# Layer-2 feed-forward: four of a token's six expert rows summed by TensorE, two added by VectorE, none by GpSimd

## The chip, the cores and the metric

The kernel runs on one core of a Trainium2 chip. A core has five engines that work side by side, each with its own queue of instructions that it takes in order: TensorE (PE in the profile, with its weight loads as PEld), VectorE (DVE), ScalarE (ACT), GpSimd (POOL) and SyncE (SP), which here only starts transfers. Transfers run on 16 DMA engines. The on-chip memory for operands is SBUF; TensorE writes its products to PSUM, which has eight banks here, and VectorE and ScalarE read them from there. The metric is the device time of one execution in microseconds (us), taken as the median of several runs.

## The reference, cut to what matters

The program is a stack of four layers on 1024 tokens of 256 numbers (4 sequences of 256), all in 32-bit floating point. Every layer has the form "half a feed-forward, attention, half a feed-forward", each on a normalised copy of the running sum x. The change is in layer 2's feed-forward, which runs twice, before and after layer 2's attention. It is a mixture of 64 experts; each token goes to its six best, and one shared expert takes all tokens:

```python
x = x + 0.5 * _L2_ffn_ref(_layernorm(x), ...)       # and again after the attention

scores = softmax(xf @ gate_w.T)
topk_w, topk_idx = top_k(scores, 6)
# the tokens of each expert are gathered (at most 64 an expert)
gu = einsum('ech,ehi->eci', gx, gate_up_proj)
g, u = split(gu, 2)
eo = einsum('eci,eih->ech', silu(g) * u, down_proj) * buf_w[..., None]
routed = zeros.at[buf_tok].add(eo)                    # six rows a token are added up
shared = (silu(xf @ shared_gate_w.T) * (xf @ shared_up_w.T)) @ shared_down_w.T
return routed + shared
```

So every token ends with x + 0.5 * (the sum of its six expert rows + the shared expert's row). How those six rows are added is what the change is about.

## The kernel before

The running sum lies in SBUF all the time as eight tiles of 128 tokens by 256 numbers, `m.x[0]` to `m.x[7]`; tiles 0 to 3 are half 0, tiles 4 to 7 half 1. `m.xT` holds the normalised and transposed copy of each half, as TensorE's operand. `norm_steps` (L169) makes it: per tile the statistics (`st`, L176, and `mv`, L177), per half a chain of small steps on VectorE for the reciprocal root (`rsqrt`, L155), then per tile the normalised rows `xn` (L185), two transposes by TensorE (L136) and a copy.

`l2_ffn` (L868) works in these steps.

- The norm, the router's scores, the six best experts of a token and the lists of slots.
- Sixteen groups of four experts (`experts`, L954), eight of them in flight at a time: an indirect transfer by GpSimd fetches rows of tokens (L971), TensorE makes the gate and up products (L990) and the down products, and an indirect transfer by GpSimd writes each result row to its place in a table in DRAM, `parts` (L1019). A token's six rows lie side by side there.
- The shared expert (L1028 to L1034), in two halves of 512 tokens: `gated` (L193) makes two blocks of gate and up products and their product `hs` on VectorE (L203); then for each of four tiles a down product of two accumulating steps goes into a PSUM bank `accb` (two such banks), and VectorE adds half of it to x (`add_to_x`, L208, which is L209 in the profile).
- The collection (L1035 to L1045): for each of the eight tiles a transfer on SP's queue reads the 128 x 6 x 256 numbers of `parts` into a buffer `got` (L1037; four buffers), once all scatters have landed. GpSimd adds rows 3, 4 and 5 to rows 0, 1 and 2 in one instruction over 128 x 768 elements (L1043). VectorE then adds half of each of the three remaining rows to x, three `add_to_x` in all.

After the first call comes layer 2's attention (`l2_attn`), which starts with the norm of both halves. After the second call come layer 3's feed-forward and attention, half by half, the second half begun some turns after the first (`staggered`, L1783).

The kernel is written with a framework (Tile) that puts in all semaphores and hands out the buffers. It also sets the order of each engine's queue, once, when the program is built: it plans the whole program with its own estimate of each instruction's duration and takes, for each engine, what it believes to be ready, the earlier written first. No order is written by hand in these lines. On the chip an engine then keeps to this order, even where its next instruction waits and a later one could run. The names of buffers are those of the profile: `got`, `x`, `accb`, `hs`, `parts`.

A product of 32-bit numbers shows in the trace as two instructions of TensorE.

Of the kernel before, what the change touches and what calls it, by code (L numbers as in the profile page):

```python
# [10 lines left out]
F32 = mybir.dt.float32  # L11
# [3 lines left out]
ALU = mybir.AluOpType  # L15
# [4 lines left out]
P = 128  # L20
B, S, D = 4, 256, 256
# [846 lines left out]
def l2_ffn(m, w, tables, beside=None):  # L868
# [4 lines left out]
    nc, io = m.nc, m.io  # L873
    E, K = 64, 6
    table, parts = tables
    with ExitStack() as ctx:
# [72 lines left out]
        wk = pool("l2f", 2)  # L949
# [78 lines left out]
        for half in range(2):  # L1028
            cols = lambda f: slice(f * 96, f * 96 + 96)
            h = m.gated(wk, half, lambda k, f: w.sg[:, k, cols(f)], lambda k, f: w.su[:, k, cols(f)], [96] * 2, "hs")  # L1030
            for q in range(4):
                o = m.acc_bank()
                m.mm(o[:, :D], [(h[f][:96, q * P : (q + 1) * P], w.sd[:, f, :]) for f in range(2)])
                m.add_to_x(half * 4 + q, o[:, :D], 0.5)  # L1034
        for t in range(NT):  # L1035
            got = wk.tile([P, K, D], F32, name="got", bufs=4)
            ins = nc.sync.dma_start(  # L1037
                out=got.rearrange("p k d -> p (k d)"),
                in_=parts[t * K * P : (t + 1) * K * P, :].rearrange("(p k) d -> p (k d)", k=K),
            )  # L1040
            for s in scattered:
                m.tc.add_manual_dep(ins.ins, s.name, written, reason="any expert may have written these rows")
            nc.gpsimd.tensor_tensor(got[:, :3], got[:, :3], got[:, 3:], ALU.add)  # L1043
            for k in range(3):
                m.add_to_x(t, got[:, k], 0.5)  # L1045


def l2_attn_weights(m, wk):
# [684 lines left out]
def program(tc, io):  # L1733
    with ExitStack() as ctx:
# [4 lines left out]
        with tc.tile_pool(name="small2", bufs=1) as small2:  # L1739
            with slots() as m.wts:  # L1740
                with tc.tile_pool(name="small1", bufs=1) as m.small:
                    with tc.tile_pool(name="l1w", bufs=2) as stage:
                        with m.banks(4, 2, 2):
                            with tc.tile_pool(name="l0w", bufs=1) as wk:
                                with tc.tile_pool(name="l0i", bufs=1) as early:
                                    w0, rest = l0_weights(m, wk, early)
                                wa, parts = l1_attn_weights(m, stage)
                                w1 = l1_ffn_weights(m)
                                next(parts)
                                l0_ffn(m, w0, rest)  # L1750
                        with m.banks(0, 2, 2):
                            l0_attn(m, w0, parts)
                    with tc.tile_pool(name="l2w", bufs=1) as stage:
                        m.small = small2
                        m.causal = m.table(stage, "causal")
                        zero = stage.tile([P, D + 64], F32, name="zero")
                        nc.gpsimd.memset(zero, 0.0)
                        (w2, turned), (wb, more) = l2_ffn_weights(m, stage), l2_attn_weights(m, stage)
                        with m.banks(4, 2, 2):
                            l0_ffn(m, w0)  # L1760
                            l1_ffn(m, w1)
                        with m.banks(0, 2, 2):
                            tables = l2_tables(m, zero)
                            l1_attn(m, wa, chain(turned, more))
                    with m.banks(4, 2, 2):
                        l1_ffn(m, w1)
                with m.banks(4, 2, 2):
                    l2_ffn(m, w2, tables[0])
            with m.banks(6, 0, 2):
                l2_attn(m, wb)  # L1770
            with m.banks(4, 2, 2), tc.tile_pool(name="small3", bufs=1) as m.small:
                late = []
                with tc.tile_pool(name="wts", bufs=5) as m.wts:
                    l2_ffn(m, w2, tables[1], lambda: late.extend((l3_ffn_weights(m), l3_attn_weights(m))))
                w, wa = late
                with ExitStack() as pools:
                    pool = lambda name, bufs: pools.enter_context(tc.tile_pool(name=name, bufs=bufs))
                    one, wf, wk = pool("l3a1", 1), pool("l3f", 2), pool("l3a", 4)
                    l3_attn_tables(m, wa, one)
                    layer = lambda half: chain(  # L1780
                        l3_ffn(m, w, wf, half), l3_attn(m, wa, wk, half), l3_ffn(m, w, wf, half)
                    )
                    staggered((layer(half) for half in range(2)), 2, 14)  # L1783
# [40 lines left out]
```

## Time and profile before

| | |
|---|---|
| median of 3 runs | 2099.32 us (2096.6 to 2113.83) |
| the profiled execution, time | 2095.15 us |
| its span, first to last instruction | 2093.4 us |
| TensorE busy (PE) | 1816.7 us, 87% |
| VectorE busy (DVE) | 1198.1 us, 57% |
| ScalarE busy (ACT) | 707.4 us, 34% |
| GpSimd busy (POOL) | 578.1 us, 28% |
| mean granted clock of TensorE | 0.914 of full |
| collection in call 1, first load issued to last add | 964.8 to 999.5 us |
| collection in call 2, first load issued to last add | 1852.7 to 1887.9 us |
| one load of `got`, issue to landing (median) | 4.3 us for 768 KB |

All durations come from one execution, recorded by the hardware profiler. Times in a view count from the start of its span. In a line of the timeline the first number is the start, the second the time that the group took, then come engine, line of the kernel, operation, out<-in, shapes, and how many instructions were merged; in brackets stands how long the engine was idle before it, and what ended that wait. A busy share of an engine is an average over the whole program; what a change in one stage is worth has to be read in that stage. "PEclk" or "granted clock" is the clock that TensorE was allowed, as a share of full speed. The chain of waits names, step by step and backwards from the end, what each piece of work had waited for. A wait for several things is put down to the one that came last.

### The profile page before, as it was taken

Reading aid. Unit: us, or ns where it says so; the run is one execution under the profiler, and the core shown is the slowest. Engines: PE = TensorE matmul, PEld = TensorE weight load, DVE = VectorE, ACT = ScalarE, POOL = GpSimd, SP = SyncE. Lnnn points to the kernel's source line nnn. Section 1 sums busy time; section 2 is a strip of 40 time slices with the busy share of each in tenths; the row PEclk is TensorE's granted clock in tenths of the full one; section 3 lists DMA queues with packets and bytes.
Section 4 is the critical chain, followed back from the end, with each engine's and each line's share of the span. In section 5 each row is a group of like instructions: output and inputs, shape, how many; then the busy total and the mean of one; then the engine's idle time right before and its main releaser. Section 6 shows DMA issues by size and latency. Waiting matters only on the chain. (4 is left out here: it accounts for less than half of the span.)

```text
span 2093.4 us, 33728 instructions
## 1 busy us (share of the span) xinstructions
PE 1816.7 (87%) x12924; PEld 1184.3 (57%) x12924; DVE 1198.1 (57%) x2910; ACT 707.4 (34%) x1573; POOL 578.1 (28%) x1128
## 2 busy tenths in 40 slices
PE   3979999998998999487659999999999967877888
PEld 2445655466556566353336677667777754534555
DVE  8653434333555433545778887788765653464562
ACT  7325521101545211121324554544545531211210
POOL 0023200001323000176334435334333232751110
PEclk9976899999999999698769999999999986988999
DMA  8001002235000213295120111111011045950000
GB/s 232 3 10 41 11 19 61 86 106 167 1 1 1 81 41 81 84 298 194 48 82 22 42 42 52 32 52 37 17 37 38 15 114 153 302 190 0 1 3 18
DMA packets 121872, 147.38 MB, mean 70 GB/s; under 512 B 18008, under 2 KB 95472, under 8 KB 121712
## 3 DMA queue, kind: packets, MB, share of 16 engines
q1 hardware_dynamic: 113488, 123.72, 19.6%
q0 software_dynamic: 6144, 18.88, 2.9%
q10 hardware_dynamic: 2080, 2.62, 0.3%
q8 instruction: 103, 1.69, 0.3%
q14 instruction: 57, 0.47, 0.1%
HBM read 120.03 MB, written 25.17 MB: 69 GB/s over the span
## 5 line engine op out<-in xcount | busy, mean ns | idle before, releaser
L132 PE MATMUL mmb<-xT,slot 128*128 128x512 f32 (+2 forms) x640 | 285.8, 603 | 2.0 <-DVE h L203 1.0
L132 PEld LDWEIGHTS mmb<-xT,slot 128*128 128x128 f32 (+2 forms) x640 | 118.3, 188 | 151.6 <-issue 144.7
L209 DVE SCALAR_TENSOR_TENSOR x<-accb,x 128x256 f32<-128x256 f32 x112 | 47.0, 421 | 195.4 <-PE accb L132 195.3
L132 PE MATMUL accb<-slot,h 128*128 128x256 f32 (+2 forms) x640 | 145.3, 384 | 0.0
L132 PEld LDWEIGHTS accb<-slot,h 128*128 128x128 f32 (+2 forms) x640 | 119.0, 190 | 28.5 <-issue 13.9
L1175 DVE SCALAR_TENSOR_TENSOR qT<-mmb,l_conv,qT 128x510 f32<-128x510 f32 (+2 forms) x96 | 70.8, 738 | 58.5 <-ACT qT L1171 57.6
L590 ACT ACTIVATE sg<-mmb 128x512 f32<-128x512 f32 (+1 forms) x56 | 33.4, 597 | 199.2 <-PE mmb L132 196.3
L144 ACT COPY xT<-trb 128x256 f32<-128x256 f32 x44 | 16.3, 371 | 201.3 <-PE trb L136 175.5
L971 POOL DMA_INDIRECT rows<-table,source x64 | 61.9, 968 | 75.0 <-ACT l_ffn L1549 36.1
L772 POOL TENSOR_TENSOR e<-e,den 128x512 f32<-128x512 f32 x64 | 51.5, 826 | 109.4 <-DVE den L769 106.3
L1175 DVE SCALAR_TENSOR_TENSOR vT<-mmb,l_conv,vT 128x510 f32<-128x510 f32 (+2 forms) x96 | 71.2, 741 | 18.1 <-ACT vT L1171 17.2
L1221 POOL TENSOR_TENSOR put<-lt,t_same 32x128 f32<-32x128 f32 x128 | 63.9, 499 | 27.3 <-DVE lt L1216 20.5
L720 POOL TENSOR_TENSOR x<-x,l_bo 128x256 f32<-128x256 f32 x8 | 6.5, 832 | 230.7 <-DVE xn L185 230.7
L1000 DVE SCALAR_TENSOR_TENSOR h<-sg,rows,mmb 64x96 f32<-64x96 f32 x128 | 40.0, 313 | 50.9 <-ACT sg L995 48.8
L592 DVE TENSOR_TENSOR sg<-sg,c 128x512 f32<-128x512 f32 x44 | 30.8, 701 | 67.0 <-ACT sg L590 51.2
L1019 POOL DMA_INDIRECT parts<-os,target x64 | 63.0, 984 | 19.9 <-issue 12.7
L1175 DVE SCALAR_TENSOR_TENSOR kT<-mmb,l_conv,kT 128x510 f32<-128x510 f32 (+2 forms) x96 | 66.3, 735 | 1.9 <-ACT kT L1171 1.7
L990 PE MATMUL mmb<-slot,gx 128*64 128x192 f32 x512 | 61.7, 361 | 6.3 <-DVE gx L142 5.7
L132 PE MATMUL mmb<-xT,wq 128*128 128x512 f32 x128 | 67.1, 649 | 0.0
L132 PE MATMUL accb<-wo,zT 128*128 128x256 f32 x256 | 60.9, 391 | 6.0 <-DVE x L209 4.4
L132 PE MATMUL mmb<-xT,l_ffn 128*128 128x512 f32 x128 | 64.3, 653 | 1.2 <-DVE xT L142 1.2
L136 PE MATMUL trb<-t_ident,xn 128*128 128x128 f32 x144 | 31.6, 343 | 38.3 <-DVE xn L185 31.3
(452 smaller groups left out, 4336.4 us busy)
## 6 DMA issues: line engine op xcount, KB each, us to landing
slot<-_L_ffn_gate_up_proj_dram SPq DMA_DIRECT2D x16, 1536.0 KB, 8.7
slot<-in_L_ffn_down_proj_dram SPq DMA_DIRECT2D x8, 1536.0 KB, 14.4
parts<-zero SPq DMA_DIRECT2D x16, 768.0 KB, 9.5
got<-parts SPq DMA_DIRECT2D x16, 768.0 KB, 4.3
bca<-scr SPq DMA_DIRECT2D x32, 256.0 KB, 3.1
bcb<-scr SPq DMA_DIRECT2D x32, 256.0 KB, 3.2
c<-rows SPq DMA_DIRECT2D x16, 256.0 KB, 3.2
table<-xs ACTq DMA_DIRECT2D x2, 1280.0 KB, 5.1
```

The source lines that it names most:

```text
L132: self.nc.tensor.matmul(out=out, lhsT=a, rhs=b, start=i == 0, stop=i == last, **kw)
L136: self.nc.tensor.transpose(out, in_, self.ident[:n, :n])
L209: self.nc.vector.scalar_tensor_tensor(self.x[t], got, scale, self.x[t], ALU.mult, ALU.add)
L590: nc.scalar.activation(sg[:n], g[:n], AF.Silu)
L592: nc.vector.tensor_tensor(sg, sg, c, ALU.mult)
L772: nc.gpsimd.tensor_tensor(e[:, :, cut], e[:, :, cut], den[:, i, :].unsqueeze(2).to_broadcast([P, 2, n]), ALU.mult)
L971: nc.gpsimd.indirect_dma_start(out=r, out_offset=None, in_=table, in_offset=bass.IndirectOffsetOnAxis(ap=slot[0][:, 2 * g + i : 2 * g + i ...
L990: nc.tensor.matmul(out=ps[half, i, :], lhsT=xT[:, i, k, half], rhs=gu[:, 4 * (g % 2) + 2 * i + j, k, :], start=k == 0, stop=k == KC - 1,)
L1000: nc.vector.scalar_tensor_tensor(h[half, i, :], sg[half, i, :], rows[i][half, D + e : D + e + 1], ps[half, i, 96:], ALU.mult, ALU.mult,)
L1019: ins = nc.gpsimd.indirect_dma_start(out=parts, out_offset=bass.IndirectOffsetOnAxis(ap=slot[1][:, 2 * g + i : 2 * g + i + 1], axis=0), in ...
L1175: nc.vector.scalar_tensor_tensor(yi[:, :, d:], ps[:, :, : S - d], tap(j), yi[:, :, d:], ALU.mult, ALU.add)
L1221: nc.gpsimd.tensor_tensor(batches[b].put[rows(q), :, :, u * G : u * G + G], lt[rows(q), :, rows(q)].rearrange("p c (z t) -> p t z c", z=2) ...
```

## The change

In the collection, GpSimd's addition is taken out. For each tile TensorE now multiplies rows 2, 3, 4 and 5 by the identity matrix (`m.ident`, 128 x 128), all four accumulating in one PSUM bank `accb`; that bank then holds their sum. VectorE adds half of rows 0 and 1 to x, and half of the bank. `got` has five buffers instead of four.

```diff
         for t in range(NT):
-            got = wk.tile([P, K, D], F32, name="got", bufs=4)
+            got = wk.tile([P, K, D], F32, name="got", bufs=5)
             ins = nc.sync.dma_start(
                 out=got.rearrange("p k d -> p (k d)"),
                 in_=parts[t * K * P : (t + 1) * K * P, :].rearrange("(p k) d -> p (k d)", k=K),
             )
             for s in scattered:
                 m.tc.add_manual_dep(ins.ins, s.name, written, reason="any expert may have written these rows")
-            nc.gpsimd.tensor_tensor(got[:, :3], got[:, :3], got[:, 3:], ALU.add)
-            for k in range(3):
+            o = m.acc_bank()
+            m.mm(o[:, :D], [(m.ident, got[:, k]) for k in range(2, K)])
+            for k in range(2):
                 m.add_to_x(t, got[:, k], 0.5)
+            m.add_to_x(t, o[:, :D], 0.5)
```

## The prediction

> **What bounds the kernel now.** The page comes first: TensorE is busy for 87% of the 2093.4 us span, so over the whole kernel it is the bound. The change touches two short stretches only, the ends of the two layer-2 feed-forwards, so I then read the timeline of those (965 to 1008 us, 1852 to 1890 us). The first, with columns start, duration, engine, line, operation, count and, in brackets, the idle time before and its releaser:
>
> ```profile
> 969.31 1.80 POOL L1043 TENSOR_TENSOR got<-got 128x768 f32<-128x768 f32 x1 [5.38 <-DMA got<-parts]
> ...
> 972.10 7.70 POOL L1043 TENSOR_TENSOR got<-got 128x768 f32<-128x768 f32 x4 [0.99 <-DMA got<-parts]
> ...
> 972.41 0.42 DVE L209 SCALAR_TENSOR_TENSOR x<-accb,x 128x256 f32<-128x256 f32 x1
> ...
> 974.19 5.89 DVE L209 SCALAR_TENSOR_TENSOR x<-got,x 128x256 f32<-128x256 f32 x3 [0.62 <-POOL got L1043]
> ...
> 980.68 0.67 DVE L203 TENSOR_TENSOR hs<-sg,mmb 96x512 f32<-96x512 f32 x1
> ...
> 981.40 2.07 PE L132 MATMUL accb<-l_sd,hs 96*128 96x256 f32 x4 [7.15 <-DVE hs L203]
> ...
> 998.07 0.41 DVE L185 TENSOR_SCALAR xn<-x,mv,rs 128x256 f32<-128x256 f32 x1
> ```
>
> Three VectorE adds take 5.89 us, 1.96 us each, exactly while GpSimd's four adds run; an add that reads PSUM in the same stretch takes 0.42. Behind them in VectorE's queue waits the product hs, and TensorE stands for 7.15 us for it. So this stretch is bound by VectorE, and VectorE is held by GpSimd. The spread of the two kinds of add (min/median/max in ns, from the views of the tiles got and accb) says the same:
>
> ```profile
> L209 DVE SCALAR_TENSOR_TENSOR x<-got,x x48: 401/425/2030, 971.1 to 1887.5; 128x256 f32<-128x256 f32 x48
> L1043 POOL TENSOR_TENSOR got<-got x16: 1790/1867/2054, 969.3 to 1878.1; 128x768 f32<-128x768 f32 x16
> ```
> ```profile
> L209 DVE SCALAR_TENSOR_TENSOR x<-accb,x x8: 405/416/424, 965.3 to 991.1; 128x256 f32<-128x256 f32 x8
> ```
>
> The windows (busy time of PE, PEld, DVE, ACT and POOL, then granted clock, DMA share, GB/s) show TensorE without work and its clock at half as a consequence:
>
> ```profile
> 975.00:980.00 5.00, 0.00 (x0) 0.00 (x0) 4.93 (x3) 0.00 (x0) 4.80 (x3) 0.91 0.20 75
> 980.00:985.00 5.00, 2.37 (x5) 1.47 (x6) 4.76 (x13) 0.00 (x0) 0.63 (x1) 0.50 0.69 238
> ```
>
> Last, the waits of the DMA queue: a fifth load waits until an old buffer's adds are done.
>
> ```profile
> SPq L1037 <- DVE x L209: 18.1, 4, 7.1
> ```
>
> **The change, part by part.** Per call there are eight tiles of 128 tokens.
>
> *GpSimd's add goes.* In call 1 the stretched adds are 5.89 us for three (1.28 unstretched, at 425 ns) and 1.89, 1.67 and 1.61 for one each: 4.6 + 1.5 + 1.2 + 1.2 = 8.5 us too long. In call 2 they are 4.32 for three, 1.25, 1.89, 2.95 for three, and two tiny norm steps of 1.71 and 1.76: 3.0 + 0.8 + 1.5 + 1.7 + 1.5 + 1.6 = 10.1 us. The first add of each call also no longer waits for GpSimd's 1.8. The ceiling of this term is 8.5 + 1.8 + 10.1 + 1.8 = 22 us, if nothing else becomes the bound.
>
> *VectorE's own count stays.* Three adds a tile before (three row sums), three after (two rows, one PSUM sum), and a PSUM add costs 416 ns against 425. Nothing.
>
> *TensorE gets 32 products a call*, four a tile, two instructions each. The trace has no product with the identity over 256 columns; the nearest row is the layer-3 down product of the same shape (128x128 by 128x256), 64 instructions in 13.83 us, from the chain; the row at half clock is the shared expert's:
>
> ```profile
> 1905.93 13.83 PE accb L132 x64
> ```
> ```profile
> 1877.72 3.78 PE L132 MATMUL accb<-l_sd,hs 96*128 96x256 f32 x8 [0.56 <-DVE x L209]
> ```
>
> That is 0.216 us an instruction, 1.73 us a tile, 13.8 us a call at full clock; at half clock 0.47, 3.8 a tile, 30 a call. I take the full clock, because with products to do TensorE has no gap as long as the 5 us that halved it at 979; the other end goes to a rival. This is the term that takes most of the ceiling back. The weights' loads (0.19 us) lie beneath the products.
>
> *What the path becomes.* Each engine's queue is in order. In TensorE's, the shared expert's products are written ahead of the identity products and are always ready first, so I expect all eight sums behind them.
>
> Call 1: the gate and up products end at 974.25, as now. VectorE's hs for the second half is queued behind the adds of about four tiles. The loads' landings: first 969.2, second 972.1, and the DMA engines stay full until 975.5, so the fourth is there at about 976. So hs ends at about 977.3; four shared down products at 0.9 us (the rows at full clock) end at 981; four sums end at 988.1, eight at 995.0. From the last add's end to the first normalised tile it takes 0.42 + 3.96 us (statistics at 1000.36 to xn at 1004.32 now). Half 0 is normalised from 992.5 instead of 998.07, half 1 from 999.4 instead of 1004.32: **-5 us**, since layer 2's attention needs both.
>
> Call 2: gate and up end at 1864.9, loads land earlier (the first at 1857.1, four by 1862.3), so hs ends near 1865.5, shared products 1869.4, four sums 1876.3, eight 1883.2. Half 0 could be normalised from 1880.7 instead of 1884.80, but its transposes stand behind the last sums: 1883.3 instead of 1885.27, -2.0. The clock then stays up: layer 3's first products ran at 0.50 from 1890.07 to about 1893.6, which lost 1.8. **-3.8 us**.
>
> *VectorE's two row adds now wait for the load alone.* Now the first three come right behind the first two shared adds, though GpSimd's 1.8 us lies before them. Freed of it they may be queued ahead of these shared adds. A second new wait is the third add's for TensorE's sum; behind it stand hs and the norm's steps, which the sums above include. If the row adds go ahead, the shared adds wait for the landing: 969.2 + 0.85 instead of 965.26, 4.8 us in call 1, and 1857.1 + 0.85 instead of 1855.94, 2.0 us in call 2; TensorE's next shared product waits for the bank. That leaves -0.2 and -1.8. So the two ends are -8.8 and -2.0, and with the queue order unknown I take **-5**.
>
> *The fifth buffer.* A buffer is now freed by TensorE's sum as well, later than by VectorE. From the release to the landing is 4.3 us (median of the load); TensorE takes 6.9 us over the other four, so five buffers hide it and four would (5.2) only just. It costs nothing on the path; with one tile as cover it would be 4.3 - 1.7 = 2.6 us for each of three loads. Queued behind the loads in SP's queue are three small tables in call 1, whose first reader is at 992.7 and off the path.
>
> *Sum.* On the profiled execution: 2095.15 (span 2093.4) - 5 = **2090**. The median of the runs shown, 2099.32, is 4 above it, so a median of 2094 would say the same; that stays inside the range.
>
> [...] The clock: in call 1 TensorE stopped at 974.25 and the granted clock fell at 979.5; in call 2 it stood from 1864.94 to 1868.47, 3.5 us, and the next burst of 1.13 still ran at full clock, with half clock from 1870. [...]
>
> **The rivals.**
> 1. *The queues come out ideally*: hs is not behind late loads, TensorE never waits. From 963.5, 14.5 us of shared work and 6.9 for four sums give 984.9, and half 1's end at 991.7: half 1 is normalised from 996, -8.3; call 2 gets to about -6.5, and the attention starts with the clock up, -1. That is 2079; up to the ceiling of 22, with the queues later in the kernel also falling well, 2073. For it: TensorE is idle for 20 of the 43 us from 965 to 1008. Against it: eight sums make TensorE this stretch's bound.
> 2. *TensorE is the new bound at half clock: slower.* If the first row adds stand ahead of the shared adds, TensorE is idle from about 967 to 970 and again for hs; from a gap above 5 us (the one at 974) the clock is at half, and a tile's sum costs 3.8 instead of 1.73: +2.1 x 8 = 17 us a call until some 4 us of unbroken work restore it (1890.07 to 1893.6). For both calls without restoring +34 - 2 = +32, 2127; with restoring half-way about +15, 2110. For it: the shared down products run at half clock now, in both calls. Against: the sums are unbroken work, once started.
> 3. *The order moves elsewhere.* A new ready time in one stage can change the queues of what follows, 708 us of attention (64 of them without TensorE work) and 203 of layer 3 (31). Either sign; I bound it by a tenth of that idle time gained, and by twice as much lost: -10 to +20, 2080 to 2110.
> 4. *Nothing comes of it*: the sums end when GpSimd's adds did; 2095. The equality of 13.8 us of sums and 8 x 1.8 = 14.4 of GpSimd speaks for it, TensorE's idle time against.
>
> **How the numbers follow.** The forecast, with its own ends of 2086 and 2093, 40; rival 1 and the good half of 3, 19; rival 4, 16; rival 2 and the bad half of 3, 25. The range that leaves out a tenth on each side is 2070 to 2114. A per cent is 21 us, about what a measurement of this kernel tells from no change. Faster by more takes nearly the ceiling plus a better order later: 16 in 100. Slower by more takes half clock in both calls or a worse order later: 20. Within: 64.
>
> **What would show it.** In the profile of the changed kernel no row add should be above 0.45 us, GpSimd's line should be gone, and 64 identity instructions a call should take 13.8 us. If they take near 30, rival 2 holds. The idle time before hs and before the shared down products tells whether row adds stand ahead of them; the starts of xn in both calls give the two terms, and the time from there to the end tells rival 3. The prediction is wrong if that last stretch moves by more than 10 us, or if TensorE takes sums ahead of shared products and waits for loads.

## The result, and the profile after

The changed kernel takes 2109.41 us (median of 20 runs, 2101.41 to 2121.38), the kernel before beside it 2101.61 us (20 runs): a ratio of 1.0036, 95% interval 1.002 to 1.0053. That is 7.6 us slower (4.2 to 11.1), where 5 us faster was forecast. The two profiled executions lie further apart, 2117.6 against 2095.15 us, because one execution is not a median: the stretch ahead of the first call, in which nothing was changed, took 863.1 us in one and 852.8 in the other.

What GpSimd had done to VectorE is gone, as the view of the tile got shows (min/median/max in ns):

```profile
L132 PE MATMUL accb<-got,t_ident x128: 378/379/634, 993.6 to 1910.9; 128*128 128x256 f32 x128
L209 DVE SCALAR_TENSOR_TENSOR x<-got,x x32: 407/424/426, 980.3 to 1909.5; 128x256 f32<-128x256 f32 x32
```

No row add is above 426 ns; before, the longest took 2030. The timeline of the first call, lines of VectorE, TensorE and SP taken together, to be held against the first one shown of before (this execution is 10.8 us later when the shared expert begins):

```profile
976.03 0.86 DVE L209 SCALAR_TENSOR_TENSOR x<-accb,x 128x256 f32<-128x256 f32 x2 [0.79 <-PE accb L132]
...
980.31 0.88 DVE L209 SCALAR_TENSOR_TENSOR x<-got,x 128x256 f32<-128x256 f32 x2 [3.43 <-DMA got<-parts]
981.12 0.42 DVE L209 SCALAR_TENSOR_TENSOR x<-accb,x 128x256 f32<-128x256 f32 x1
...
985.24 0.68 DVE L203 TENSOR_TENSOR hs<-sg,mmb 96x512 f32<-96x512 f32 x1
...
985.97 1.13 PE L132 MATMUL accb<-l_sd,hs 96*128 96x256 f32 x4 [0.95 <-DVE hs L203]
...
987.58 0.68 DVE L203 TENSOR_TENSOR hs<-sg,mmb 96x512 f32<-96x512 f32 x1
...
988.31 5.49 PE L132 MATMUL accb<-l_sd,hs 96*128 96x256 f32 x12 [1.21 <-DVE hs L203]
...
993.59 11.33 PE L132 MATMUL accb<-got,t_ident 128*128 128x256 f32 x48
...
996.32 3.77 SPq L1037 DMA_DIRECT2D got<-parts  x3
...
1005.17 3.72 PE L132 MATMUL accb<-got,t_ident 128*128 128x256 f32 x16 [0.25 <-DVE x L209]
```

VectorE is no longer held, but it waits for the loads instead (3.43 us at 980.31), hs still stands behind row adds, and TensorE's last shared products run at half clock: 5.49 us for 12, 0.46 each, where the 8 at 977.12 took 1.89. The windows (busy time of PE, PEld, DVE, ACT, POOL, then the granted clock) show it:

```profile
985.00:990.00 5.00, 2.84 (x9) 1.82 (x8) 3.12 (x7) 0.00 (x0) 0.40 (x1) 0.84 0.44 165
990.00:995.00 5.00, 5.00 (x13) 4.01 (x13) 2.03 (x5) 0.00 (x0) 0.00 (x0) 0.50 0.00 0
```

The last three loads are issued at 996.32, when the first sums set buffers free. The waits of the DMA queue have a new releaser, where before it was VectorE's add (35.6 us over both calls):

```profile
SPq L1037 <- PE accb L132: 32.9, 6, 15.1
```

VectorE alone, a little later:

```profile
1002.64 0.17 DVE L179 TENSOR_SCALAR nv<-mv 128x4 f32<-128x4 f32 x1
1003.90 0.43 DVE L209 SCALAR_TENSOR_TENSOR x<-got,x 128x256 f32<-128x256 f32 x1 [1.08 <-DMA got<-parts]
...
1009.22 0.73 DVE L185 TENSOR_SCALAR xn<-x,mv,rs 128x256 f32<-128x256 f32 x2
...
1015.34 0.73 DVE L185 TENSOR_SCALAR xn<-x,mv,rs 128x256 f32<-128x256 f32 x2
```

The norm of half 0 has begun (nv), and then VectorE stands for the load of a tile of half 1, whose row adds are queued in the middle of the norm's steps. The line at 1015.34 is the first of half 1's normalised rows. In the second call (TensorE's timeline) there is no half clock, and layer 3's products begin at full clock (granted 1.00 from 1890 to 1928.5):

```profile
1892.73 4.22 PE L132 MATMUL accb<-l_sd,hs 96*128 96x256 f32 x16
1896.78 10.53 PE L132 MATMUL accb<-got,t_ident 128*128 128x256 f32 x48
1907.56 3.72 PE L132 MATMUL accb<-got,t_ident 128*128 128x256 f32 x16 [0.24 <-DVE x L209]
...
1914.24 13.97 PE L132 MATMUL mmb<-xT,l_ffn 128*128 128x512 f32 x32 [0.61 <-DVE xT L142]
```

Cut into stretches by the starts of instructions: a collection from the shared expert's first product to the first product of what follows, attention from its first product (tile l_ab) to the router's scores of the second call.

| us | first collection | attention | second collection | layer 3's first up products |
|---|---|---|---|---|
| before | 50.85 | 714.59 | 42.81 | 15.70 |
| after | 51.11 | 725.45 | 39.03 | 13.81 |

The first collection gained nothing, the second with layer 3's start 5.7 us. And attention, whose instructions are the same in the same order on every engine, took 10.9 us more. The second call's experts, unchanged too, took 131.3 us against 125.2. Is that the chance of one execution, or does it come with the change?

### The profile page after: what moved, and what is told of

Same layout as the page of the kernel before. It is cut to its first block, busy times and chain, and to the rows that moved or that the text cites. A ratio compares the mean times of both kernels' runs of the same rounds, so it can differ in the third digit from the quotient of the medians.

```text
span 2115.9 us, 33958 instructions
## 1 busy us (share of the span) xinstructions
PE 1856.6 (88%) x13052; PEld 1215.1 (57%) x13052; DVE 1183.3 (56%) x2910; ACT 708.3 (33%) x1573; POOL 549.0 (26%) x1112
## 5 line engine op out<-in xcount | busy, mean ns | idle before, releaser
L209 DVE SCALAR_TENSOR_TENSOR x<-accb,x 128x256 f32<-128x256 f32 x128 | 54.0, 422 | 211.5 <-PE accb L132 211.4
L1000 DVE SCALAR_TENSOR_TENSOR h<-sg,rows,mmb 64x96 f32<-64x96 f32 x128 | 40.1, 313 | 54.1 <-ACT sg L995 51.9
L132 PE MATMUL mmb<-xT,wv 128*128 128x512 f32 x128 | 64.6, 627 | 0.0
## 6 DMA issues: line engine op xcount, KB each, us to landing
slot<-_L_ffn_gate_up_proj_dram SPq DMA_DIRECT2D x16, 1536.0 KB, 14.3
```

The costliest lines, as they stand in the source:

```text
L132: self.nc.tensor.matmul(out=out, lhsT=a, rhs=b, start=i == 0, stop=i == last, **kw)
L209: self.nc.vector.scalar_tensor_tensor(self.x[t], got, scale, self.x[t], ALU.mult, ALU.add)
L1000: nc.vector.scalar_tensor_tensor(h[half, i, :], sg[half, i, :], rows[i][half, D + e : D + e + 1], ps[half, i, 96:], ALU.mult, ALU.mult,)
```

## The experiments

They ran on chips on which the kernel before takes 2141 to 2146 us, since both stretches of experts are longer there (128 to 130 and 142 to 152 us, against 104 and 125). So a ratio is always against runs of the kernel before on the same chip; differences in us are the ratio on 2144. One profile's stretch outside the collections scatters by several us, so kernels are read there in groups.

**Fifth buffer, sums, and the ceiling.** Theory A: the extra time arises outside the collections, with the clock; B: the sums on TensorE cost it; C: the fifth buffer does.

pool_five_buffers, the kernel before with one buffer more:

```diff
-            got = wk.tile([P, K, D], F32, name="got", bufs=4)
+            got = wk.tile([P, K, D], F32, name="got", bufs=5)
```

> The kernel before with only the fifth buffer (GpSimd still adds three rows). Measured from the first shared gate product to the first product of the stage that follows, the collection took 50.9 us in call 1 and 42.8 us in call 2 before, 51.1 and 39.0 after. Theory A (the instruction order outside the two collections is the same in both kernels; the collections did not get slower, and the extra time of the changed kernel arises outside them, from when TensorE's clock is halved): the fifth buffer alone gives 49 to 51 and 41 to 43, and the total is within 0.2% of the kernel before or spreads as its runs do. Theory B (the identity sums on TensorE cost the time): the same here, total 0 to -0.2%. Theory C (the fifth buffer costs, through later transfers or buffer places): call 1 above 52 and the total 0.2 to 0.5% up.

Measured: 1.0001 (0.9982 to 1.0019).

sum_four_buffers, the changed kernel with four buffers:

```diff
-            got = wk.tile([P, K, D], F32, name="got", bufs=5)
+            got = wk.tile([P, K, D], F32, name="got", bufs=4)
```

> The changed kernel with four buffers. The fifth load then waits for the first tile's sum on TensorE, about 20 us after the first load. Theory A: the collections grow by 2 to 4 us each (53 to 55 and 41 to 43 us), since VectorE's norm stands behind the adds of a later load, and the total is 0.2 to 0.4% above the changed kernel's. Theory C: the total falls back to that of the kernel before.

Measured: 1.0034 (1.0016 to 1.0052), as with five, and the collections take 50.78 and 40.81 us: the growth that theory A expected here didn't come. C is out; of A and B these runs don't decide. Seven buffers, with which only the eighth load would wait for a sum, do not fit beside the rest in SBUF (83.5 KB a partition for 79.8 left), so what the late loads cost by themselves is not measured.

three_rows_only, the kernel before without GpSimd's add; rows 3, 4 and 5 are left out of the sum:

```diff
-            nc.gpsimd.tensor_tensor(got[:, :3], got[:, :3], got[:, 3:], ALU.add)
```

> The kernel before without GpSimd's addition and with nothing in its place: three of the six expert rows are left out of the sum. It is the ceiling of taking GpSimd away. Prediction's term: 22 us for both calls, so the collections at about 40 and 32 us and the total 0.7 to 1.0% below the kernel before. Theory A allows that the total falls by less than the collections do. Theory B: the total falls by the full 20 us, since then only the sums had taken it back.

Measured: 0.99 (0.987 to 0.9931), -21 us; the collections take 41.90 and 30.97 us. So GpSimd's add costs what the prediction's ceiling of 22 us said, and how the three rows are added otherwise decides what is left of it.

**One call at a time.** Theory L: the loss comes with the first call, the second call gains. Four buffers in both.

```diff
+            if beside is None:        # sum_call_1_only; "is not None" in sum_call_2_only
                 o = m.acc_bank()
                 m.mm(o[:, :D], [(m.ident, got[:, k]) for k in range(2, K)])
                 for k in range(2):
                     m.add_to_x(t, got[:, k], 0.5)
                 m.add_to_x(t, o[:, :D], 0.5)
+            else:
+                nc.gpsimd.tensor_tensor(got[:, :3], got[:, :3], got[:, 3:], ALU.add)
+                for k in range(3):
+                    m.add_to_x(t, got[:, k], 0.5)
```

> The first call's collection is that of the change (four rows by TensorE, two by VectorE), the second call's that of before (GpSimd's add back); four buffers. Theory L (the loss is local and comes with the first call): its collection gains nothing (0 to +1 us, as in the profile of the change), and the expert stretch of the second call, whose instructions are the same, grows by 5 to 6 us, so about +6 us, ratio 1.003. Rival M (that growth belongs to the second call's change, or was chance): within 1.5 us of before, ratio 1.000.

Measured: 1.0028 (1.0011 to 1.0046), +6 us.

> The second call's collection is that of the change, the first call's that of before; four buffers. Theory L: only the gain of the second call is left, -3.8 us in its collection and -1.9 in layer 3's up products, so about -5.7 us, ratio 0.9973, and everything up to the second collection takes what it took before. Rival M: the second call's expert stretch or the last stretch grows here, 0 to +5 us, ratio 1.000 to 1.0025.

Measured: 0.998 (0.9962 to 0.9998), -4 us. L holds in its totals: the first call's change loses time, the second's gains some. The two make +2 us, while both with four buffers made +7; each of these has some 4 us of uncertainty. But the place of the loss was wrong. The experts of the second call take 147.31 us with the first call's change and 146.82 without it, and the first collection (48.49) is no longer than before. Attention differs: 720.85 against 714.34.

**Other splits of the six rows.** vector_six lets VectorE add all six, with four buffers; sum_three and sum_two let TensorE sum the last three or two, VectorE the others and the bank, with five:

```diff
-            nc.gpsimd.tensor_tensor(got[:, :3], got[:, :3], got[:, 3:], ALU.add)
-            for k in range(3):
+            for k in range(K):                                               # vector_six
                 m.add_to_x(t, got[:, k], 0.5)
```
```diff
-            m.mm(o[:, :D], [(m.ident, got[:, k]) for k in range(2, K)])
-            for k in range(2):
+            m.mm(o[:, :D], [(m.ident, got[:, k]) for k in range(3, K)])     # sum_two: 4
+            for k in range(3):
```

> GpSimd's add goes and TensorE adds nothing: VectorE adds all six rows; four buffers. Against the kernel with three rows left out (-21.8 us) VectorE has 24 more adds of 0.425 us a call, 10.2 us, if all stand on the path: -1.4 us; as far as they lie beside TensorE's shared products and the loads, less. If TensorE's sums are what takes GpSimd's gain back, this is faster than before by 2 to 12 us, ratio 0.994 to 0.999. If VectorE's queue with its row adds in front is what costs, it is no faster than before: 0 to +8 us.

Measured: 0.9992 (0.9977 to 1.0007). Its adds are as short as the changed kernel's, but there are 96 of them, and 48 more than with three rows cost nearly all of the 21 us, as expected if all of them stand on the path:

```profile
L209 DVE SCALAR_TENSOR_TENSOR x<-got,x x96: 404/417/429, 993.9 to 1925.5; 128x256 f32<-128x256 f32 x96
```

> TensorE sums three rows instead of four (24 products a call, 10.4 us at full clock instead of 13.8), VectorE adds three rows and the bank; five buffers. If the length of TensorE's sums sets the end of the collection, 3.4 us less a call than the change: 0 to -1 us against before, ratio 1.000. If the number of VectorE's adds sets it, 8 x 0.42 = 3.4 us a call more than the change: about +14 us, ratio 1.0065.

Measured: 0.997 (0.9954 to 0.9985), -6 us: faster than both kernels, and by more than the shorter sums explain, since its first collection takes 49.72 us, within the 47.4 to 51.5 of the kernels that sum four rows there. Attention is the difference again: 716.91 us.

> TensorE sums two rows (16 products a call, 6.9 us), VectorE adds four rows and the bank; five buffers; 64 instructions more a call, a quarter of a block. By the work alone it lies between VectorE adding all six (0.9992) and TensorE summing three (0.997): 0.996 to 0.999. If the limits of the instruction blocks are what sets such small differences, attention's length shows it: 714 to 719 us and a ratio in that range, or 721 and above and a ratio of 1.000 to 1.003.

Measured: 0.9981 (0.9956 to 1.0006), attention 713.74.

**Where attention loses it.** Lay the attentions over each other from their first product, and every kernel so far with four rows summed in the first call falls behind in the same places. One of them in the changed kernel (TensorE's timeline):

```profile
1211.43 0.28 PE L132 MATMUL accb<-st,qa 128*128 128x128 f32 x1
1213.06 0.38 PE L132 MATMUL accb<-st,qa 128*128 128x128 f32 x1 [1.35 <-issue]
```

These are the two instructions of one product. The timeline shows nothing between them, and the profile names nothing that was waited for ("issue"). Yet TensorE stands for 1.35 us, and then the clock falls, to 0.5 at 1213.7. The windows of the changed kernel and, at about the same work, of the one before:

```profile
1209.00:1212.00 3.00, 2.68 (x137) 2.20 (x135) 2.98 (x8) 0.73 (x3) 0.95 (x4) 1.00 0.02 5
1212.00:1215.00 3.00, 1.94 (x11) 1.91 (x11) 2.27 (x9) 0.50 (x2) 1.13 (x2) 0.78 0.36 93
1215.00:1218.00 3.00, 3.00 (x22) 1.72 (x21) 2.21 (x11) 1.37 (x5) 1.22 (x6) 0.65 0.24 82
```
```profile
1195.00:1198.00 3.00, 3.00 (x145) 2.64 (x143) 2.67 (x6) 2.10 (x6) 1.87 (x5) 1.00 0.00 0
1198.00:1201.00 3.00, 3.00 (x40) 2.58 (x35) 2.93 (x6) 1.28 (x3) 1.91 (x2) 1.00 0.21 68
1201.00:1204.00 3.00, 3.00 (x9) 1.33 (x8) 2.73 (x15) 1.36 (x4) 0.47 (x3) 1.00 0.33 113
```

The list of DMA queues of the changed kernel (packets, MB, share) has a queue that no line of the kernel issues to:

```profile
q8 instruction: 104, 1.70, 0.3%
```

104 packets of 16 KB, and TensorE's record has 13052 matmul instructions and 13052 weight loads: about 251 a packet, and with the 481 instructions that only wait, 256. The kernel before has 256 of these records fewer, and 103 packets. So it looks as if TensorE's instructions came in blocks of 256, an estimate from these counts. The change puts 32 products into a call, 64 instructions with as many weight loads: 128, half a block. Everything behind the first call lies half a block further on. In the trace each of these stops lies within 2 us of a packet of this queue, in stretches where TensorE runs through 128 matmul instructions of 32x32 by 32x16 and their weight loads in 1.4 to 1.7 us. That alone proves little, since packets there follow each other every 3.5 to 4 us. Theory F is that the shift makes TensorE run out of instructions where it didn't before; rival S, that the sums do it themselves.

pad_before and pad_after add 32 tiny products to the kernel before and to the changed one, as many instructions as the sums and next to no work, into a bank that nobody reads:

```diff
             for k in range(3):
                 m.add_to_x(t, got[:, k], 0.5)
+        if beside is None:
+            o = m.acc_bank()
+            m.mm(o[:32, :16], [(m.ident[:32, :32], m.ident[:32, :16])] * 32)
```

> The kernel before with 32 tiny products (32 x 32 by 32 x 16, into a bank that nobody reads) at the end of the first call's shared expert: as many TensorE instructions as the change adds there (64 products and 64 weight loads as they show in the trace), but only about 0.7 us of work; the rest stands in the same order on every engine. Theory F (TensorE's instructions are loaded in blocks of 16 KB; 128 instructions more shift the blocks' limits by half a block, and in layer 2's attention TensorE then runs out of instructions in other places): attention takes 721 to 725 us instead of 714 to 719, with idle times of 1.2 to 1.6 us that nothing releases at about 192, 228 and 252 us after its first product, as in the three kernels that sum four rows in the first call; total +5 to +8 us, ratio 1.0025 to 1.0035. Rival S (the sums themselves, or the state in which they leave the engines, make the attention longer): attention as before, total +0.7 us, ratio 1.000.

Measured: attention 724.77 us; total 1.0013 (0.9992 to 1.0034). The two stops of about a microsecond or more that TensorE's waits list from 175 to 265 us of attention are there (columns: waited for, us in total, times, longest):

```profile
PE mmb L132 <- issue: 1.6, 1, 1.6
...
PE accb L132 <- issue: 0.9, 1, 0.9
```

The changed kernel has 1.4 and 1.4 in the same stretch, the kernel before none. The third that was expected, at 228 us, isn't there: the wait of 1.2 us near it is one for VectorE, which the kernel before has too. The total moved less than expected, +3 us (-2 to +7), which by itself is not clear of nothing.

> The changed kernel with the same 32 tiny products more at the end of the first call, so that its first call has 256 instructions of TensorE more than before, a whole block of 16 KB. Theory F: attention has the blocks of the kernel before again, 714 to 719 us, without the idle times at 192, 228 and 252 us; total at least 4 us below the changed kernel, ratio to before 0.998 to 1.0015 (the gain of the second call, about -5 us, less what the first call's longer stretch costs). Rival S: as the changed kernel or 0.7 us above it, 1.0035.

Measured: attention 718.28 us, no such stop in that stretch, full clock where the changed kernel lost it:

```profile
1221.00:1224.00 3.00, 3.00 (x128) 2.65 (x128) 2.41 (x6) 2.21 (x6) 2.07 (x6) 1.00 0.02 5
1224.00:1227.00 3.00, 3.00 (x75) 2.79 (x64) 2.96 (x6) 0.97 (x3) 1.67 (x2) 1.00 0.15 51
```

Total 0.9974 (0.9951 to 0.9997), -6 us: with work added that does nothing, the changed kernel becomes faster than both.

A control has the same products at the end of the second call (`is not None`), so that the program is as long, but attention's blocks stay where the change put them; beside it ran the changed kernel itself.

> The changed kernel itself, beside the next one on one chip. Theory F: attention 721 to 725 us with idle times at about 192, 228 and 252 us after its first product; ratio 1.002 to 1.005.

Measured: 1.0021 (1.0003 to 1.0038), attention 722.71, with a stop inside the same product:

```profile
1219.72 0.38 PE L132 MATMUL accb<-st,qa 128*128 128x128 f32 x1 [1.09 <-issue]
```

> The changed kernel with the 32 tiny products at the end of the second call's collection instead of the first's: the program is as long as with them in the first call, but in attention the blocks of TensorE's instructions are those of the changed kernel. Theory F: attention 721 to 725 us with the idle times at about 192, 228 and 252 us; ratio to before as the changed kernel's, 1.002 to 1.006. Rival P (any such products, or a program of that length, do what they did in the first call): attention 714 to 719 us, ratio 0.996 to 0.999.

Measured: 1.0026 (1.0006 to 1.0046), attention 725.91, the stop again:

```profile
1229.03 0.38 PE L132 MATMUL accb<-st,qa 128*128 128x128 f32 x1 [1.09 <-issue]
```

Rival P is out: it isn't the products, it is where they stand. That TensorE waits for its instructions to be loaded fits all this, but no view shows the wait itself; what the runs show is the count. All fourteen profiles by the instructions that the first call adds:

| added in call 1 | attention, us |
|---|---|
| none: before, pool_five_buffers, sum_call_2_only, vector_six, three_rows_only | 714.59, 718.95, 714.34, 717.75, 719.90 |
| a whole block: pad_after | 718.28 |
| a quarter, three eighths: sum_two, sum_three | 713.74, 716.91 |
| half a block: after, after_again, sum_four_buffers, sum_call_1_only, pad_before, pad_after_call_2 | 725.45, 722.71, 721.62, 720.85, 724.77, 725.91 |

No kernel of the last row is below any of the others: means of 723.6 and 716.8, 6.8 us. In all six, and in no other, the clock is at half for 3.4 or 6.8 us from about 250 to 257 us on.

The two places show it more sharply than the sums. Each start of an instruction of TensorE was held against the same one of the kernel before: from 190 to 205 us of attention the six of the last row fall behind by 1.0 to 3.3 us, from 245 to 262 us by another 3.1 to 4.9; the others by no more than 0.3 and 0.5. That is 5.5 of the 6.8 us. At the first place a stop alone cost 1.0 to 1.4 us (four kernels), a stop with half clock behind it 3.2 and 3.3 (two).

## Why the prediction was wrong

**What bounded the stretch, and the ceiling: right.** GpSimd held VectorE; three_rows_only gave -21 us where the sum of stretched adds said 22.

**TensorE's part: right.** 64 instructions took 11.33 + 3.72 = 15.1 us in call 1 and 10.53 + 3.72 = 14.3 in call 2, predicted 13.8, and they stand behind all shared products. Rival 2, sums at half clock, came in call 1 for the first four instructions only: the clock fell before them, at 988.4, and rose at 995.2.

**Call 1, "-5 us": wrong by nearly all of it.** Up to hs the steps hold: it ends at 988.26, predicted 977.3, with 10.8 for the later start 988.1. Then two steps failed. The shared down products behind hs were put at full clock, because only a gap like the 5 us of before would halve it; they ran at half, behind gaps of 0.95 and 1.21 us. They end at 993.8 instead of 991.8, and the sums, themselves 1.1 longer, at 1008.9 instead of 1005.8. And VectorE's part behind the sums was reckoned as if nothing lay between: half 0 was normalised at 1009.2 instead of 1003.3, 5.9 late. Of this 2.6 come from the later sums; for the rest the steps took 7.3 us from the last add instead of 3.96, since VectorE's queue has seven adds of half 1 amid them, the first of which waits 1.08 us for a load that itself waited for a sum. So "five buffers hide it" holds for TensorE, which had other tiles to sum, and not for VectorE, whose next instruction was one of those row adds. Half 1, which attention needs as well, was normalised at 1015.3 instead of 1010.2, 5.1 late: 3.1 from the sums, 2 from half 0's late rows and copies among its own steps. That takes the whole of the 5 us back. That four buffers give the same total as five (1.0034, 1.0036) agrees with "it costs nothing" for the fifth, not with its reason. Over all profiles the first collection takes 50.2 us with GpSimd's add (four profiles) and 49.7 with the four-row sums (six, 47.4 to 51.5): -0.5, within the scatter.

**Call 2, "-3.8 us": right.** The second collection and layer 3's up products take 58.8 us in the four profiles with GpSimd's add and 54.1 in the five with the sums and nothing else: -4.7; sum_call_2_only's total is -4.3. The clock stayed up as forecast: the second collection has 20 to 23 us of half clock in those four and none in these five. Both collections together give -5.2. That this is the forecast's number is luck: the forecast chose -5 between -8.8 and -2.0, and call 1 gave next to nothing.

**The sum, "2095.15 - 5": this is the step that decided.** It put the rest of the kernel at nothing, and rival 3 let it move only if "the order moves elsewhere". The order didn't move; the count of TensorE's instructions ahead of attention did, by 128, and attention lost 6.8 us. -5.2 and +6.8 make +1.6. The runs show more: +7.6 and +4.5 for the changed kernel, each with some 3.5 us of uncertainty, and 128 instructions more in call 1 take 10 to 13 us away, with some 6. So 3 to 6 us have no place yet. The second call's experts may hold some of it (mean 148.0 us in the five half-block profiles of these chips, 145.9 in the other seven; 131.3 against 125.2 in the first two profiles), but the two groups overlap there, and it stays open.

**"Wrong if that last stretch moves by more than 10 us"** named the danger, and the profile showed it at once. Without the experiments it could not be told from the scatter of unchanged code, which was 10 us in the stretch ahead of the change.

## What to carry to other kernels

Less than a microsecond of work cost or saved microseconds elsewhere by the count of its instructions alone: 32 tiny products, about 0.7 us by an estimate from the 128 instructions of their shape that take 1.4 to 1.7, made attention 724.77 us instead of 714.59 in the kernel before and 718.28 instead of 725.45 in the changed one. Where a long program runs dense stretches of tiny instructions, look at TensorE's waits "on issue" and at the instruction queue's packets before and after, and try the same change with some empty products beside it. Measure a change that is worth less than half a per cent with such a shifted twin before it is called good or bad: here the split of the rows (sum_three, 0.997) and the padding (pad_after, 0.9974) both turned a loss into a gain. And a buffer that is "hidden" must be hidden from whatever is queued behind its reader, not from the path alone: here the row add amid the norm's steps waited 1.08 us for its load.

## What was not expected of the hardware

- TensorE stood still for 0.9 to 1.6 us with nothing that the profile shows to wait for, even between the two instructions of one product (1.35 us before 1213.06 in the changed kernel), and where this fell depended on how many instructions came before: with half a block more it was there (pad_before 1.6 and 0.9 us, pad_after_call_2 1.2 and 1.1), with a whole block not (pad_after). That it waits for its own instructions is the reading that fits; no view shows that wait. The instruction queue moved 104 packets of 16 KB for some 26600 records of TensorE, about 256 a packet.
- Such a stop could be followed by half clock for 3.4 or 6.8 us in the granted clock, though the stop itself was short. At about 252 us of attention all six kernels show it, behind stops of 1.2 to 1.6 us; at about 192 us two of them, behind 1.35 and 1.62, and not the four with 0.9 to 1.2. Where the changed kernel stood for 1.35 us it fell 3.2 us behind the kernel before, so there the clock cost more than the stop. The delay differed: the clock fell 0.6 us after that stop of 1.35 us had ended, in call 2 of the kernel before 1.5 us after the end of one of 3.5, and in call 1 of the kernel before at 979.1 (the forecast has 979.5), 4.9 us into a gap that began at 974.25. How long a stop must be for the clock to fall these runs don't show.
